# A graph attention layer on one core: TensorE's products in another order within a step

## The chip, the cores and the metric

One core of one Trainium2 chip runs the kernel. A core has TensorE (PE: matmuls and turnings; its weight loads are listed apart as PEld), VectorE (DVE), ScalarE (ACT), GpSimd (POOL) and SyncE (SP), each with an instruction stream of its own that runs in order. DMA transfers are issued from SP, ACT and POOL. PE works on a grid that can be used whole or cut into tiles (64 or 32 rows or columns); the profile writes the tile's shape beside each product (`64*128`: 64 rows, 128 columns). Matmul results land in PSUM, which has eight banks; one bank holds 512 float32 for each of 128 partitions.

The metric is the device time of one launch in microseconds (us).

## The reference, cut to what matters

12500 nodes with 128 channels, 400000 edges sorted by target; `edge_dst` is skewed (its density falls with the node's number).

```python
h = relu(layernorm(x))
msg_src = h @ w_src + b_src
msg_dst = h @ w_dst
message = msg_src[edge_src] + msg_dst[edge_dst]
rad_w = silu(silu(edge_scalars @ w1 + b1) @ w2 + b2) @ w3 + b3     # 32 -> 64 -> 64 -> 128
message = message * edge_attr * rad_w
message = message @ w_sep + b_sep                                  # 128 -> 256
msg_h = message.reshape(n_edges, 8, 16 + 16)
alpha, value = smooth_leaky_relu(msg_h[:, :, :16]), msg_h[:, :, 16:]
score = einsum('ehk,ahk->eh', alpha, alpha_dot)
att = segment_softmax(score, edge_dst)                             # by target node
out = segment_sum(value * att, edge_dst).reshape(n_nodes, 128)
return x + out @ w_proj + b_proj
```

## The kernel before

Three parts follow one another. The first computes the two node tables `t_src` and `t_dst` in DRAM (to about 113 us). The second, `windows()`, goes over the edges in 400 steps of 1000 edges and is nearly the whole run. The third divides, projects and adds the residual (the last 85 us or so).

Within `windows()`, a step `k` handles two sections (f = 0, 1) of 500 edges; a section is four tiles of 125 edges. `step(k)` is a list of calls written by hand; the scheduler is off (`tc.manual_schedule()`), so each engine carries out its instructions in the order in which the calls stand. What a step does, with the lines of the kernel before:

- `gather` (L744, POOL): four indirect DMAs a section fetch the 125 source rows of each tile from `t_src` into `gs0` or `gs1`, each with two buffers. The indices stand in `idx`.
- `sources` (L808, PE): turns the four tiles of a section into PSUM bank `pm0` or `pm1`. `message` (L816, PE) adds the target rows to the same banks: a one-hot matrix `ohT` (L788, DVE) times the window's rows `md`, split into three bfloat16 parts `m3` (`split_md`: L730 and L735 on ACT, L733 and L737 on DVE).
- the radial network: `e_T` (L754) turns the edge scalars, `mlp1` (L763), `mlp2` (L778) and `mlp3` (L795) are products on PE with a silu on ACT between them (L766, L781); L799 (DVE) adds the bias and multiplies by the edge weight: `rad`. Then L821 (DVE) makes the message `mT` from `pm` and `rad`.
- `alphas` (L825 PE, L827 ACT, L829 DVE), a section at a time, through the one bank `pa`.
- `scores` (L836 PE, L839 ACT) every second step, for two steps at once. The scores of eight steps go to DRAM (`sc_d`, L841) and come back laid out by heads (`S`, L846).
- the softmax of a group of eight steps: a scan upwards (L857), one downwards (L862), a subtraction (L867) and an exponential (L869), then four turnings (`softmax_T`, L880) into `Pem`.
- `values` (L908 PE, L910 DVE): `mT` of step c times `w_v`, in bank `V`, times the softmax's numerators, into `pvx`. `one_hot` (L895, L898, DVE) builds the matrix `oh` of the window's targets; `sums` (L919 PE, L923 ACT) adds up by target; `store_win` and `store` (L927, L931, SP) write the result to DRAM.

Values lag the message by LAG = 12 steps (`c = k - LAG`), because the softmax of eight steps must be complete first. PSUM's eight banks are `p3` (two), `pm0`, `pm1`, `V`, `pa`, `misc` and `m1`, each with one buffer; whoever fills a bank waits until its last reader is done. `p3` is shared by all three layers of the radial network, `misc` by scores, sums, `softmax_T` and the index turnings (`prep_make`, L697).

After step 399 the group's last steps run in a tail of LAG + 2 steps, with jobs between them that join windows (`jobs`, from step 401 on).

Of the kernel before, what the change touches and what calls it, by code (L numbers as in the profile page):

```python
# [21 lines left out]
F32 = mybir.dt.float32  # L22
# [30 lines left out]
LAG = 12  # L53
# [3 lines left out]
def gnn_kernel(ctx: ExitStack, tc: tile.TileContext, a: dict, out: bass.AP):  # L57
# [603 lines left out]
    def windows():  # L661
# [5 lines left out]
        with tc.tile_pool(name="wk2", bufs=2) as sp, tc.tile_pool(name="ps", bufs=1, space=PSUM) as pp, \  # L667
# [3 lines left out]
            eTs, h1s, h2s, ohT, m3, mr, mTs, als, S_all, sms, Ps, Pem, pvx, ohs, accs, xs, Ms, pms = (  # L671
                {} for _ in range(18))
# [15 lines left out]
            def prep_make(u):  # L688
                ri, rb = prep[u]
                rows = lp.tile([P, 2, T], F32, name="rows", bufs=1)  # L690
                rf = lp.tile([P, 1], F32, name="rf", bufs=1)
                nc.vector.tensor_copy(rf, rb)
                nc.vector.tensor_copy(rows[:, 0, :], ri[:, 0, :])
                nc.vector.tensor_scalar(rows[:, 1, :], ri[:, 1, :], rf, None, op0=ALU.subtract)
                pt = pp.tile([T, 2, P], F32, name="misc")
# [6 lines left out]
                nc.vector.tensor_copy(loc, pt[:, 1, :])  # L702
                prep[u] = (idx, loc)
# [87 lines left out]
            def mlp3(k):  # L791
                p3 = pp.tile([C, 2, BANK], F32, name="p3")
                for f in range(2):
                    s = slice(f * FC, (f + 1) * FC)
                    nc.tensor.matmul(p3[:, f, 0:SEC], w3b[s, :], h2s[k][s, :], start=True, stop=True)  # L795
                rad = sp.tile([C, PR], F32, name="rad", bufs=1)
# [4 lines left out]
                return rad  # L801
# [9 lines left out]
            def message(k, rad):  # L811
                pm = [pms.pop((k, f)) for f in range(2)]
                for j in range(3):
                    for f in range(2):
                        s = slice(f * W, (f + 1) * W)
                        nc.tensor.matmul(pm[f], m3[k][s, j, :], ohT[k][s, :], start=False, stop=(j == 2),  # L816
                                         skip_group_check=True)
                mTs[k] = sp.tile([C, PR], F32, name="mT", bufs=LAG + 1)
                for f in range(2):
                    s = slice(f * SEC, (f + 1) * SEC)  # L820
                    nc.vector.scalar_tensor_tensor(mTs[k][:, s], pm[f], b_n, rad[:, s], op0=ALU.add, op1=ALU.mult)  # L821

            def alphas(k, f):
                pa = pp.tile([C, SEC], F32, name="pa")
                nc.tensor.matmul(pa, w_a, mTs[k][:, f * SEC:(f + 1) * SEC], start=True, stop=True)  # L825
# [59 lines left out]
            def weights(c):  # L885
                pvx[c] = sp.tile([T, 2, TS, ROW], F32, name="pvx")
                q = c % MP * 2
                for f in range(2):
                    nc.scalar.copy(pvx[c][:, f, :, C:ROW], Pem[c // MP][:, :, q + f, :])

            def one_hot(c):
                _, loc = prep[c // 16]
                ohs[c] = sp.tile([T, 8, W], F32, name="oh")
# [58 lines left out]
            prep_make(0)  # L952
            for k in range(2):
                load_e(k)
            def step(k):
                c = k - LAG
                if has(c - 1):
                    store_win(c - 1)
                    store(c - 1, 0)
# [11 lines left out]
                if has(c - 1):  # L971
                    store(c - 1, 1)
# [3 lines left out]
                if k % 16 == 8 and has(k + 8):  # L976
                    prep_make((k + 8) // 16)
# [5 lines left out]
                if has(k + 1):  # L983
                    split_md(k + 1, 0)
                if has(c):
                    weights(c)
                rad = mlp3(k) if has(k) else None
# [179 lines left out]
            for k in range(NP, NP + LAG + 2):  # L1167
# [167 lines left out]
```

## Time and profile before

| what | us |
|---|---|
| median of 3 runs (4452.02 to 4453.61) | 4452.02 |
| the profiled execution | 4452.25 |
| its span, first to last instruction | 4450.5 |
| first gather starts, last gather starts | 118.7, 4232.1 |
| PE busy | 4148.3 |
| POOL busy | 3117.5 |
| DVE busy | 3083.0 |
| ACT busy | 1957.6 |
| mean granted TensorE clock | 0.981 |

How it is read: busy time is the time in which an engine carried out instructions; the issuing of DMAs by SP and ACT, register work and waits are not in it. A row of a group of instructions gives their line, engine, operation, the tiles written and read, how many there are, then their busy time, the mean of one in ns, and the engine's idle time just before them with what ended it. `issue` means that the profile shows nothing that the engine waited for. In an order of time a row is a start, a length, an engine, a line and an operation, with the idle time before it in brackets.

### The profile page before, as it was taken

The page shows a single profiled execution, that of the slowest core. Times are in us where ns is not written, and L with a number is a line of the kernel's source. Part 1 is how long each engine was busy: PE and PEld are TensorE (multiplying, and loading weights), DVE is VectorE, ACT ScalarE, POOL GpSimd, SP SyncE. Part 2 cuts the span into 40 slices and gives each one's busy share as a digit, 9 for nine tenths or more (in the row PEclk, how much of TensorE's full clock was granted, in tenths as well). Part 3 has the DMA queues.
Part 4 walks back from the last instruction along what each step waited for, and adds up shares of the span by engine and source line. Part 5 has one row for each costly group of instructions (what it writes and reads, how often), then busy time and mean ns, then how long its engine had stood idle before and what let it go on. Part 6 is the DMA issues. An engine that isn't in the chain of part 4 may idle for free.

```text
span 4450.5 us, 87691 instructions
## 1 busy us (share of the span) xinstructions
PE 4148.3 (93%) x29692; PEld 2314.3 (52%) x29692; DVE 3083.0 (69%) x6005; ACT 1957.6 (44%) x4595; POOL 3117.5 (70%) x3223
## 2 busy tenths in 40 slices
PE   6689999999999999999999999999999999999964
PEld 4245555555555555555555555555555555555553
DVE  6367777776776777777777777767767677777666
ACT  5244444444444444444444444444444444444421
POOL 0767777777777777777777777777777777777701
PEclk9799999999999999999999999999999999999987
DMA  5767777777777777777777777776776777777624
GB/s 208 202 179 173 183 186 177 187 184 181 187 178 188 187 178 187 188 177 185 189 177 187 186 172 180 178 178 178 172 183 177 175 181 178 173 182 178 169 51 183
DMA packets 601335, 794.74 MB, mean 179 GB/s; under 512 B 130270, under 2 KB 476974, under 8 KB 600746
## 3 DMA queue, kind: packets, MB, share of 16 engines
q1 hardware_dynamic: 394664, 520.94, 40.9%
q0 software_dynamic: 102816, 210.37, 23.7%
q10 hardware_dynamic: 103394, 57.74, 5.1%
q8 instruction: 234, 3.83, 0.4%
q14 instruction: 227, 1.86, 0.1%
HBM read 648.39 MB, written 140.67 MB: 177 GB/s over the span
## 4 chain that ended last, share of the span: by engine, by line
PE 80%; DVE 8%; ACT 5%; DMA 4%; issue 3%; SPq 1%; POOL 0%; ACTq 0%; POOLq 0%; DVEq 0%
PE V L908 16%; PE pa L825 15%; PE misc L919 8%; PE p L795 8%; PE pm L808 8%; PE pm L816 6%; PE p L763 5%; PE misc L836 5%; PE p L778 4%; PE m L754 2%; ACT sl L827 2%; DVE al L829 2%; DVE M L862 1%; DMA agg<-ob 1%; DVE mT L821 1%
## 5 line engine op out<-in xcount | busy, mean ns | idle before, releaser
L744 POOL DMA_INDIRECT gs<-t_src,idx x3200 | 3103.1, 970 | 1127.8 <-issue 838.5
L827 ACT ACTIVATE sl<-pa,c_b_a 128x500 f32<-128x500 f32 x800 | 543.0, 679 | 1764.4 <-PE pa L825 1760.8
L799 DVE SCALAR_TENSOR_TENSOR rad<-p,c_fc_b,w_b 128x500 f32<-128x500 f32 x800 | 553.3, 733 | 541.0 <-PE p L795 537.7
L829 DVE SCALAR_TENSOR_TENSOR al<-pa,sl 128x500 f32<-128x500 f32 x800 | 543.1, 679 | 551.6 <-ACT sl L827 530.3
L825 PE MATMUL pa<-mT,c_w_a 128*128 128x500 f32 x1600 | 825.4, 597 | 71.2 <-DVE al L829 38.3
L908 PEld LDWEIGHTS V<-c_w_v,mT 128*125 128x125 f32 x6208 | 735.6, 187 | 286.8 <-issue 160.8
L908 PE MATMUL V<-c_w_v,mT 128*125 128x128 f32 x6208 | 883.6, 285 | 0.3
L910 DVE TENSOR_TENSOR pvx<-V,Pem 125x512 f32<-125x512 f32 x776 | 532.0, 686 | 101.8 <-PE V L908 92.1
L821 DVE SCALAR_TENSOR_TENSOR mT<-pm,c_b_src,rad 128x500 f32<-128x500 f32 x800 | 553.1, 733 | 5.9 <-PE pm L816 5.9
L808 PEld LDWEIGHTS pm<-ident,gs 125*128 125x128 f32 x3200 | 352.9, 141 | 314.1 <-issue 251.4
L808 PE MATMUL pm<-ident,gs 125*128 125x125 f32 x3200 | 499.7, 278 | 9.3 <-DMA gs<-t_src,idx 9.3
L919 PE MATMUL misc<-pvx,oh 125*64 125x136 f32 x6400 | 463.4, 287 | 35.9 <-DVE oh L898 35.9
L919 PEld LDWEIGHTS misc<-pvx,oh 125*64 125x64 f32 x6400 | 361.1, 137 | 183.7 <-DVE oh L898 143.9
L795 PE MATMUL p<-h,w3b 64*128 64x500 f32 x1600 | 447.8, 636 | 3.1 <-ACT h L781 3.1
L816 PE MATMUL pm<-ohT,m 64*128 64x500 bf16 x2400 | 325.1, 377 | 0.0
L781 ACT ACTIVATE h<-p,b 128x500 f32<-128x500 f32 x400 | 292.0, 730 | 12.3 <-PE p L778 12.3
L825 PEld LDWEIGHTS pa<-mT,c_w_a 128*128 128x128 f32 x1600 | 239.8, 189 | 101.7 <-DVE al L829 51.9
L766 ACT ACTIVATE h<-p,b 128x500 f32<-128x500 f32 x400 | 289.8, 725 | 0.7 <-PE p L763 0.7
L763 PE MATMUL p<-eT,w1b 64*128 64x250 f32 x1600 | 278.6, 425 | 1.0 <-ACT eT L756 1.0
L778 PE MATMUL p<-h,w2b 64*64 64x250 f32 x3200 | 262.9, 399 | 13.2 <-ACT h L766 13.2
L763 PEld LDWEIGHTS p<-eT,w1b 64*128 64x128 f32 x1600 | 121.0, 185 | 296.4 <-issue 294.6
L895 DVE TENSOR_TENSOR oh<-lane,loc 125x504 f32<-125x504 f32 x400 | 275.1, 688 | 0.0
(145 smaller groups left out, 3138.5 us busy)
## 6 DMA issues: line engine op xcount, KB each, us to landing
w_b<-in_edge_weight SPq DMA_DIRECT2D x400, 500.0 KB
d_b<-in_dst SPq DMA_DIRECT2D x400, 250.0 KB
gs<-t_src,idx POOLq DMA_INDIRECT x3200
e_t<-in_edge_attr ACTq DMA_DIRECT2D x400, 125.0 KB
sc_d<-Sp SPq DMA_DIRECT2D x200, 250.0 KB
win<-ob SPq DMA_DIRECT2D x400, 68.0 KB
agg<-ob SPq DMA_DIRECT2D x800, 33.5 KB
md<-t_dst SPq DMA_DIRECT2D x800, 32.0 KB
```

What stands on the lines that cost most here:

```text
L744: nc.gpsimd.indirect_dma_start(out=gs[:, j, :], out_offset=None, in_=t_src[:, :], in_offset=bass.IndirectOffsetOnAxis(ap=idx[:, t:t + 1], ...
L763: nc.tensor.matmul(p1[:, q, 0:2 * T], w1b[s, :], eTs[k][s, :], start=True, stop=True)
L795: nc.tensor.matmul(p3[:, f, 0:SEC], w3b[s, :], h2s[k][s, :], start=True, stop=True)
L799: nc.vector.scalar_tensor_tensor(rad[:, s], p3[:, f, 0:SEC], b3, w_g[k][:, s], op0=ALU.add, op1=ALU.mult)
L808: nc.tensor.matmul(pms[k, f][:, t * T:(t + 1) * T], gs[:T, t, :], ident[:T, :T], start=(t == 0), stop=False, is_transpose=True, skip_group ...
L816: nc.tensor.matmul(pm[f], m3[k][s, j, :], ohT[k][s, :], start=False, stop=(j == 2), skip_group_check=True)
L821: nc.vector.scalar_tensor_tensor(mTs[k][:, s], pm[f], b_n, rad[:, s], op0=ALU.add, op1=ALU.mult)
L825: nc.tensor.matmul(pa, w_a, mTs[k][:, f * SEC:(f + 1) * SEC], start=True, stop=True)
L827: nc.scalar.activation(sl, pa, AF.Silu, bias=b_a, scale=1.0)
L829: nc.vector.scalar_tensor_tensor(al, pa, 0.25, sl, op0=ALU.mult, op1=ALU.add)
L908: nc.tensor.matmul(V[:, t, :], mTs[c][:, o:o + T], w_v, start=True, stop=True)
L919: nc.tensor.matmul(acc[f * W:(f + 1) * W, :], ohs[c][:, f * TS + t, :], pvx[c][:, f, t, :], start=(t == 0), stop=(t == TS - 1), skip_group ...
```

## The change

No product, vector operation or transfer is added or removed, with one exception: the first layer's silu is two operations of half the size. The order of the calls in `step(k)` is another, and with it the lags:

- `values(c, 0)` and `values(c, 1)` stand half a step apart, each followed by `alphas` of the step before (k - 1) and `sources` of this step, so that three products of the whole grid follow one another; `e_T` is put behind the second three. `mlp1` and `mlp3`, both of 64 rows, follow one another. A step changes the tile's shape six times (seven with scores).
- Both turnings of a step's sources are made in the step itself, half a step apart; before, that of f = 0 was made in the step ahead. The gathers follow them.
- `alphas` comes one step behind the message, `scores` two, `values` 13 (LAG = 13), `sums` 14. The stores follow the sums (`c - 2`), and the tail has LAG + 3 steps. The softmax's parts stand one step later within the group of eight (r = 2, 3, 4).
- `mlp1` writes into the banks `m1` and `misc` in place of `p3`, with a silu for each; `scores` goes to `m1` in place of `misc`.
- `prep_make` is cut in two: the vector operations one step earlier, the turning (`prep_turn`) where it was. `mlp3` and `alphas` are cut into their product and their DVE part (`radial`, `alphas_sum`), which are placed apart. Buffers: `al` 7 for 6, `pvx` 3 for 2.

```diff
-LAG = 12
+LAG = 13
...
-                p1 = pp.tile([P, 2, BANK], F32, name="p3")
+                p1 = [pp.tile([P, 2 * T], F32, name=n) for n in ("m1", "misc")]
                 for q in range(2):
                     s = slice(q * 2 * RAD, (q + 1) * 2 * RAD)
-                    nc.tensor.matmul(p1[:, q, 0:2 * T], w1b[s, :], eTs[k][s, :],
-                                     start=True, stop=True)
+                    nc.tensor.matmul(p1[q], w1b[s, :], eTs[k][s, :], start=True, stop=True)
                 h1s[k] = sp.tile([P, SEC], F32, name="h1")
-                nc.scalar.activation(h1s[k].rearrange("x (f p q) -> x q f p", f=2, q=2),
-                                     p1[:, :, 0:2 * T].rearrange("x q (f p) -> x q f p", f=2),
-                                     AF.Silu, bias=b12[:, 0:1], scale=1.0)
+                h1v = h1s[k].rearrange("x (f p q) -> x q f p", f=2, q=2)
+                for q in range(2):
+                    nc.scalar.activation(h1v[:, q], p1[q].rearrange("x (f p) -> x f p", f=2),
+                                         AF.Silu, bias=b12[:, 0:1], scale=1.0)
...
-                al = sp.tile([C, SEC], F32, name="al", bufs=6)
+                return pa, sl
+
+            def alphas_sum(k, f, pa, sl):
+                al = sp.tile([C, SEC], F32, name="al", bufs=7)
                 nc.vector.scalar_tensor_tensor(al, pa, 0.25, sl, op0=ALU.mult, op1=ALU.add)
...
-                ps = pp.tile([P, SEC], F32, name="misc")
+                ps = pp.tile([P, SEC], F32, name="m1")
...
-                if has(c - 1):
-                    store_win(c - 1)
-                    store(c - 1, 0)
+                if has(c - 2):
+                    store_win(c - 2)
+                    store(c - 2, 0)
...
                 if has(c):
                     weights(c)
-                rad = mlp3(k) if has(k) else None
+                    values(c, 0)
+                if has(k - 1):
+                    sl = alphas(k - 1, 0)
+                if has(k):
+                    sources(k, 0)
+                if has(k + 2):
+                    gather(k + 2, 0)
+                if has(k + 1):
+                    split_md(k + 1, 1)
+                if has(c):
+                    one_hot(c)
+                if has(k - 1):
+                    alphas_sum(k - 1, 0, *sl)
+                if has(k + 1):
+                    split_md(k + 1, 2)
+                if has(k + 2):
+                    mlp1(k + 2)
+                if has(k):
+                    mlp3(k)
+                if has(k + 1):
+                    one_hot_T(k + 1)
+                if has(k):
+                    radial(k)
+                if has(c):
+                    values(c, 1)
+                if has(k - 1):
+                    sl = alphas(k - 1, 1)
                 if has(k):
                     sources(k, 1)
                 if has(k + 2):
                     gather(k + 2, 1)
-                if has(k):
-                    message(k, rad)
-                if has(c):
-                    values(c, 0)
-                if has(k + 1):
-                    split_md(k + 1, 1)
-                if has(k):
-                    alphas(k, 0)
+                if has(k + 3):
+                    e_T(k + 3)
                 if has(k + 6) and k >= -4:
                     load_e(k + 6)
                 if has(k + 1):
-                    split_md(k + 1, 2)
-                if has(k + 2):
-                    mlp1(k + 2)
-                if has(c):
-                    values(c, 1)
-                    one_hot(c)
-
-                if has(k + 1):
-                    sources(k + 1, 0)
-                if has(k + 3):
-                    gather(k + 3, 0)
+                    split_md(k + 1, 3)
+                if has(k - 1):
+                    alphas_sum(k - 1, 1, *sl)
                 if has(k):
-                    alphas(k, 1)
+                    message(k)
+                if has(c - 1):
+                    sums(c - 1)
                 if has(k + 1):
                     mlp2(k + 1)
-                    one_hot_T(k + 1)
-                    split_md(k + 1, 3)
-                if has(c):
-                    sums(c)
-                m, r = divmod(k, MP)
+                if has(k - MP) and r == 4:
+                    softmax_T(m - 1)
+                if has(k - 2) and k % 2 == 1:
+                    scores(k - 2)
                 if has(k - MP):
-                    if r == 1:
+                    if r == 2:
                         softmax_up(m - 1)
-                    elif r == 2:
+                    elif r == 3:
                         softmax_down(m - 1)
                         softmax_exp(m - 1)
-                    elif r == 3:
-                        softmax_T(m - 1)
-                if has(k + 3):
-                    e_T(k + 3)
-                if has(k) and k % 2 == 1:
-                    scores(k)
...
-            for k in range(NP, NP + LAG + 2):
+            for k in range(NP, NP + LAG + 3):
```

More of the change, by code (lines that the diff above doesn't have):

```diff
@@ L670, in windows @@
             prep, e_g, d_g, w_g, md, gath = {}, {}, {}, {}, {}, {}
-            eTs, h1s, h2s, ohT, m3, mr, mTs, als, S_all, sms, Ps, Pem, pvx, ohs, accs, xs, Ms, pms = (
-                {} for _ in range(18))
+            eTs, h1s, h2s, ohT, m3, mr, mTs, als, S_all, sms, Ps, Pem, pvx, ohs, accs, xs, Ms, pms, p3s, rads = (
+                {} for _ in range(20))
             def prep_load(u):
@@ L694, in prep_make, with prep_turn @@
                 nc.vector.tensor_scalar(rows[:, 1, :], ri[:, 1, :], rf, None, op0=ALU.subtract)
+                prep[u] = rows
+            def prep_turn(u):
+                rows = prep[u]
                 pt = pp.tile([T, 2, P], F32, name="misc")
@@ L791, in mlp3, with radial @@
             def mlp3(k):
-                p3 = pp.tile([C, 2, BANK], F32, name="p3")
+                p3s[k] = pp.tile([C, 2, BANK], F32, name="p3")
                 for f in range(2):
                     s = slice(f * FC, (f + 1) * FC)
-                    nc.tensor.matmul(p3[:, f, 0:SEC], w3b[s, :], h2s[k][s, :], start=True, stop=True)
-                rad = sp.tile([C, PR], F32, name="rad", bufs=1)
+                    nc.tensor.matmul(p3s[k][:, f, 0:SEC], w3b[s, :], h2s[k][s, :], start=True, stop=True)
+            def radial(k):
+                p3 = p3s.pop(k)
+                rads[k] = rad = sp.tile([C, PR], F32, name="rad", bufs=1)
                 for f in range(2):
@@ L809, in sources, with message @@
                                      start=(t == 0), stop=False, is_transpose=True, skip_group_check=True)
-            def message(k, rad):
-                pm = [pms.pop((k, f)) for f in range(2)]
+            def message(k):
                 for j in range(3):
@@ L815, in message @@
                         s = slice(f * W, (f + 1) * W)
-                        nc.tensor.matmul(pm[f], m3[k][s, j, :], ohT[k][s, :], start=False, stop=(j == 2),
+                        nc.tensor.matmul(pms[k, f], m3[k][s, j, :], ohT[k][s, :], start=False, stop=(j == 2),
                                          skip_group_check=True)
+                rad = rads.pop(k)
                 mTs[k] = sp.tile([C, PR], F32, name="mT", bufs=LAG + 1)
@@ L820, in message @@
                     s = slice(f * SEC, (f + 1) * SEC)
-                    nc.vector.scalar_tensor_tensor(mTs[k][:, s], pm[f], b_n, rad[:, s], op0=ALU.add, op1=ALU.mult)
+                    nc.vector.scalar_tensor_tensor(mTs[k][:, s], pms.pop((k, f)), b_n, rad[:, s],
+                                                   op0=ALU.add, op1=ALU.mult)
             def alphas(k, f):
@@ L885, in weights @@
             def weights(c):
-                pvx[c] = sp.tile([T, 2, TS, ROW], F32, name="pvx")
+                pvx[c] = sp.tile([T, 2, TS, ROW], F32, name="pvx", bufs=3)
                 q = c % MP * 2
@@ L892, in one_hot @@
                 _, loc = prep[c // 16]
-                ohs[c] = sp.tile([T, 8, W], F32, name="oh")
+                ohs[c] = sp.tile([T, 8, W], F32, name="oh", bufs=2)
                 t0 = c % 16 * 8
@@ L952, in windows @@
             prep_make(0)
+            prep_turn(0)
             for k in range(2):
@@ L970, in step @@
                     load_sm((k + 4) // MP)
-                if has(c - 1):
-                    store(c - 1, 1)
+                if has(c - 2):
+                    store(c - 2, 1)
                 if 0 <= 2 * k < NZ:
@@ L976, in step @@
                 if k % 16 == 8 and has(k + 8):
-                    prep_make((k + 8) // 16)
+                    prep_turn((k + 8) // 16)
+                if k % 16 == 7 and has(k + 9):
+                    prep_make((k + 9) // 16)
                 i, q = divmod(k - 40, MP)
@@ L984, in step @@
                     split_md(k + 1, 0)
+                m, r = divmod(k, MP)
                 if has(c):
                     weights(c)
[L987 removed]
+                    values(c, 0)
[25 more added lines that the diff above has]
+                    sl = alphas(k - 1, 1)
                 if has(k):
```

1 line of the change is left out of this document (removed).

## The prediction

> **What bounds the kernel now.** I read the page first (engine shares and the chain of waits), then POOL's gather line with all that it waited for, then PE's order of time in one step, then DVE beside POOL.
>
> From the page (shares of the span; the chain by engine; the costliest group, with its busy time, mean ns and the idle time before it):
>
> ```profile
> PE 4148.3 (93%) x29692; PEld 2314.3 (52%) x29692; DVE 3083.0 (69%) x6005; ACT 1957.6 (44%) x4595; POOL 3117.5 (70%) x3223
> PE 80%; DVE 8%; ACT 5%; DMA 4%; issue 3%; SPq 1%; POOL 0%; ACTq 0%; POOLq 0%; DVEq 0%
> L744 POOL DMA_INDIRECT gs<-t_src,idx x3200 | 3103.1, 970 | 1127.8 <-issue 838.5 <-DVE loc L702 116.5 <-PE pm L808 50.6
> ```
>
> Read alone, this says that PE is the bound and POOL has 30% to spare. The gather line by itself says otherwise (duration min/median/max, first and last start; then what ended POOL's idle time, us and times):
>
> ```profile
> L744 POOL DMA_INDIRECT gs<-t_src,idx x3200: 941/947/1537, 118.7 to 4232.1; - x189
> ...
>   issue: 838.5, 2745
> ...
>   PE pm L808: 50.6, 61
> ```
>
> 838.5 / 2745 = 0.305 us stands before every gather with no releaser, so a gather costs POOL 0.970 + 0.305 = 1.275 us. 3200 of them are 4080 us; from 118.7 to 4232.1 + 0.95 there are 4114. Only about 34 us are left in which POOL waited for PE: 50.6 less 61 x 0.305 is 32, and a row `PE misc L836: 4.8, 10` adds 1.7. In three stretches of 164 us (16 steps, 128 gathers each) POOL is busy 124.5 us on average, and 128 x 0.305 = 39.0 more makes 163.5. POOL is full, and PE is ahead of it by next to nothing: two engines bound this loop at once.
>
> PE in one step without scores (start, us, then idle time where there was any):
>
> ```profile
> 2510.34 1.11 PE L795 MATMUL p<-h,w3b 64*128 64x500 f32 x4
> 2511.38 0.65 PE L808 MATMUL pm<-ident,gs 125*128 125x125 f32 x4
> 2511.96 0.81 PE L816 MATMUL pm<-ohT,m 64*128 64x500 bf16 x6
> ...
> 2516.23 0.59 PE L808 MATMUL pm<-ident,gs 125*128 125x125 f32 x4
> 2516.66 1.01 PE L825 MATMUL pa<-mT,c_w_a 128*128 128x500 f32 x2
> ...
> 2519.26 0.43 PE L754 MATMUL m<-ident,e_t 125*128 125x125 f32 x2
> 2519.62 1.11 PE L795 MATMUL p<-h,w3b 64*128 64x500 f32 x4
> ```
>
> No idle time; 9.28 us from one L795 to the next, and 10.33 in the step before it, which has scores (2500.01 to 2510.34). The same four turnings L808 take 0.58 us between neighbours of another tile shape (64 rows) and 0.43 between neighbours of their own: 0.15 us for a change.
>
> DVE beside POOL, two pairs from one order of time:
>
> ```profile
> 4221.54 0.67 DVE L895 TENSOR_TENSOR oh<-lane,loc 125x504 f32<-125x504 f32 x1
> 4221.63 1.40 POOL L744 DMA_INDIRECT gs<-t_src,idx  x1 [0.30 <-issue]
> ...
> 4230.82 0.73 DVE L895 TENSOR_TENSOR oh<-lane,loc 125x504 f32<-125x504 f32 x1
> 4230.84 0.95 POOL L744 DMA_INDIRECT gs<-t_src,idx  x1 [0.30 <-issue]
> ```
>
> In the first the one-hot is under way when the gather starts, has 0.58 us to go, and the gather takes 0.45 us longer than 0.95. In the second both start together and the gather keeps its 0.95. The gathers' mean over their fast value, 970 - 944 = 26 ns, times 3200 is 82 us of such meetings.
>
> **The change, part by part.**
>
> *PE's order.* No product is added or taken out. A step has nine changes of shape before (ten with scores), six (seven) after: 3 x 0.15 = 0.45 us a step, 8.83 and 9.88 us, 9.36 on average. Bounds: nothing, if not the change but something else makes L808 longer, and twice as much, since L808 is short. I take 0.45. With what a group of 16 steps has besides (164 - 8 x 9.28 - 8 x 10.33 = 7 us of softmax turnings, index turnings and waits) PE then needs about 157 us for 16 steps, POOL 128 x 1.275 = 163. PE's gain of 180 us over 400 steps is therefore cut off after the 34 us that POOL waited. Two of these waits, 8.05 us at 232 and 2.10 us at 249, less 0.3 each, fall in the filling of the pipeline behind a late load and stay: **-24 us** (bounds 0 and -34).
>
> *First layer into two banks (m1, misc), two silus in place of one.* One more ACT operation a step, under 0.7 us, on an engine busy 44%: nothing. If ACT were late, the next e_T would wait, and PE has 0.4 us a step in hand.
>
> *Alphas a step later, scores two, values 13, sums 14.* Their inputs are ready a step earlier than needed; buffers grow with them (al 7, pvx 3, mT 14). SP's stores go a step later with the sums; the order of its other issues stays. Each set of four gathers is still issued right behind the turning that frees its buffer, two steps ahead of its use. Nothing in the loop.
>
> *Softmax.* The scores of a group now end at step 8m+9 and the running maximum stands at the end of 8m+10: one step, 9 us or more, for the way through DRAM, where two were. DVE stands behind that wait with the next pvx, and PE behind DVE. The trace does not show S landing. Bounds: the read is issued 2.2 us after the last score write (2449.34 and 2451.52), because it waits for that to land; and the scan found S in place 17.7 us after the scores (2449.3 and 2467.1). The read has the write's size, 250 KB, so I take another 2.2 and some room: 5 us. Cost nothing; what it costs beyond 9 us is a rival.
>
> *DVE's order.* The same operations with the same durations, but mr now stands right before the two one-hots, ohT before the radial, the scans behind mT. Their meetings with gathers fall anew. Of the operations with no PSUM operand, one of d us that meets gathers at random (pitch 1.275, the last 0.1 us free) costs (d - 0.1)^2 / 2.55: one-hot 0.688: 0.136 x 400 = 54 us; ohT 0.475: 22; the two subtractions of the split, 0.28 each: 11; 100 scans of 1.194: 47; 50 subtractions of 0.68: 7; the rest 4. Sum 145, against 82 measured: the old order met fewer than chance. Bounds: 0 (every op meets its gather as at 4230.82), and 235 (one-hot hit in full in every step, 400 x 0.588). POOL now sets the pace and PE follows landings that scatter, so meetings blur toward chance; but the ops are the measured ones, so I stay near the measured row: 90, **+8 us**.
>
> *Ends.* The last gather ends at 4233.04 and PE takes that set at 4244.03. With PE waiting for gathers the lead of 11 us falls to a landing. The very first gather, issued at 118.7, is taken at 124.46 after a wait, 4.8 us after POOL is done with it, among many other transfers; bounds 0 and 8, I take 4: -7 us. One more step in the tail is +4.6 (pm L908 at 4257.33 and 4261.97); sums there no longer wait 1.55 us for oh, which I count in the two or three early steps that no store holds, -4. Together **-6 us** (bounds -16 and +12).
>
> Sum: 4450.5 - 24 + 8 - 6 = 4428.5 us of span; the profiled run had 1.75 us around its span (4452.25), and it stands 0.2 over the median of 4452.02. Predicted 4430, 0.5% faster. From no change it can be told at 0.2%, 9 us.
>
> **The rivals.**
>
> 1. *POOL's gap is elastic* and PE's whole gain arrives: 180 us less, about 4275. For it: the chain gives PE 80% and POOL 0%. Against: 0.305 us stands before 2745 of 3200 gathers, whoever is late. 0.05.
> 2. *Meetings with DVE grow*, the other side. Place: POOL, at gathers that start under a one-hot or a scan. At chance, 145 - 82 = +63, the total is 4450.5 - 24 + 63 - 6 + 1.75 = 4485; with the one-hot locked into each step 4575. It decides from 121 us of meetings on (39 more: 24 + 6 + 9). For it: the new adjacency and pacing. Against: PE's landings scatter, 82 is the measured row. 0.20. The Trainium skill (SBUF — State Buffer, section Who interferes with whom) states that a VectorE operation with two SBUF inputs contends with GpSimd operations that read SBUF, and that the loser blocks fully. The 1.40 us gather agrees; that the gather holds off VectorE for its whole length does not show, as the one-hot at 4230.82 lost 0.06 us. By the rule alone meetings come at chance, the 4485 above.
> 3. *Softmax's maximum waits for S.* If S lands 17 us after the scores, DVE and then PE wait some 7.5 us in each group of eight steps. PE's 78.5 us a group become 86, POOL's are 81.6: 50 x 4.4 = 220 us more, about 4650. For it: two steps became one. Against: the write of the same size landed in 2.2 us. 0.05.
> 4. *PE gets no shorter* (the change does not do what it says: what L808 loses lies in weight loads, not shapes). POOL goes on waiting: 4445 to 4462. 0.12.
>
> **How the numbers follow.** Forecast 0.58, rivals as above. The forecast's own range is the collisions' 50 to 125 and the ends: 4385 to 4475. Of its 0.58, 0.47 are faster than 4443, 0.09 within, 0.02 slower; rival 1 is faster; of rival 2 0.17 are slower and 0.03 within; rival 3 slower; rival 4 0.07 within, 0.04 slower, 0.01 faster. Faster 0.53, same 0.19, slower 0.28. The range takes in rival 2 at chance and leaves out 1 and 3: 4385 to 4500.
>
> **What would show it.** Right: PE pm L814 (the turnings) waits for `DMA gs` some hundreds of times, 200 us or more in all; `PE pm L814` almost vanishes from POOL's waits; gathers 0.30 apart throughout; first to last gather about 4098. The L814 before alphas takes 0.5 us or less and a step's products sum to about 8.8 us. The gathers' mean over 944 ns, times 3200, gives the meetings: 90 or not. Wrong: POOL gaps other than 0.30 (rival 1), a mean over 980 ns (2), DVE waiting at L867 (3), no PE wait for gathers (4).

## The result and the profile after

| what | before | after |
|---|---|---|
| median (4 runs each, side by side), us | 4452.82 | 4415.2 |
| ratio to before, 95% interval | | 0.9915 (0.9897 to 0.9932) |
| span of the profiled execution, us | 4450.5 | 4414.9 |
| first gather starts, last gather ends, us | 118.73, 4233.04 | 117.27, 4208.71 |
| mean granted TensorE clock | 0.981 | 0.961 |

The changed kernel is 0.85% faster, 38 us by the medians; the prediction was 4430 us. On the page of the changed kernel the shares of the engines, the chain by engine and by line, and the two groups that matter (busy time, mean ns, idle time before and what ended most of it) read:

```profile
PE 4015.5 (91%) x29692; PEld 2440.7 (55%) x29692; DVE 3092.6 (70%) x6005; ACT 2080.8 (47%) x4995; POOL 3111.1 (70%) x3223
...
PE 57%; DMA 21%; POOL 10%; issue 6%; DVE 3%; SPq 1%; ACT 1%; POOLq 0%; ACTq 0%; DVEq 0%
DMA gs<-t_src,idx 16%; PE V L918 11%; POOL gs L748 10%; PE pa L832 9%; PE misc L929 7%; PE pm L814 6%; PE pm L821 5%; PE p L799 5%; PE m L767 4%; PE p L782 4%; PE m L846 3%; DMA agg<-ob 3%; PE m L758 1%; DMA e_t<-in_edge_attr 1%; PE misc L890 1%
...
L748 POOL DMA_INDIRECT gs<-t_src,idx x3200 | 3096.7, 968 | 1109.8 <-issue 815.9
...
L814 PE MATMUL pm<-ident,gs 125*128 125x125 f32 x3200 | 533.8, 276 | 210.6 <-DMA gs<-t_src,idx 198.8
```

The busy shares have hardly moved. The chain has: POOL and the landing of its gathers hold 26% of it, where POOL had 0% and DMA 4%. What POOL waited for in the changed kernel (us and times):

```profile
L748 POOL DMA_INDIRECT gs<-t_src,idx x3200: 938/944/1905, 117.3 to 4207.8; - x189
...
  issue: 815.9, 2675
...
  PE pm L814: 47.0, 98
```

Of the 47.0 us, 98 x 0.305 = 29.9 are the gap that stands before every gather; 17 are left, and 14.4 of these are a single wait. In the steady loop POOL no longer waits for PE. PE waits instead, as the view of PE's waits shows (us, times, longest):

```profile
PE pm L814 <- DMA gs<-t_src,idx: 198.8, 191, 5.7
```

One step of PE without scores and without a wait, in the order of time:

```profile
2503.64 1.04 PE L918 MATMUL V<-c_w_v,mT 128*125 128x128 f32 x8
2504.52 1.00 PE L832 MATMUL pa<-mT,c_w_a 128*128 128x500 f32 x2
2505.36 0.59 PE L814 MATMUL pm<-ident,gs 125*128 125x125 f32 x4
...
2506.41 1.00 PE L799 MATMUL p<-h,w3b 64*128 64x500 f32 x4
2507.34 1.14 PE L918 MATMUL V<-c_w_v,mT 128*125 128x128 f32 x8
2508.32 1.00 PE L832 MATMUL pa<-mT,c_w_a 128*128 128x500 f32 x2
...
2512.39 1.14 PE L918 MATMUL V<-c_w_v,mT 128*125 128x128 f32 x8
```

From one first `V` to the next are 8.75 us, where a step of the kernel before took 9.28. The row from which the prediction took its price, the turnings, gave little of this: from their start to the next row it is 0.52 us, where L808 between 64-row products took 0.58. More came from products that lost a neighbour of another shape: `alphas` takes 0.84 us to the next row (2504.52 to 2505.36), where it took 0.93 (2516.66 to 2517.59), and the third layer 0.93 (2506.41 to 2507.34), where it took 1.04 (2510.34 to 2511.38). Yet 16 steps still take 163.0 us on average (164.3 before), which is 128 gathers at 0.968 + 0.305 us: POOL's pace.

The one long wait of POOL has its own story, in the order of time around 260 us (SP's issues are marked SPq):

```profile
249.53 0.35 SPq L851 DMA_DIRECT2D sc_d<-Sp  x1
...
259.38 0.55 SPq L856 DMA_DIRECT2D S<-sc_d  x1
...
262.95 1.20 DVE L867 TENSOR_TENSOR_SCAN M<-sm,S 128x500 f32<-128x500 bf16 x1 [18.83 <-DMA S<-sc_d]
...
268.11 0.94 POOL L748 DMA_INDIRECT gs<-t_src,idx  x1 [14.67 <-PE pm L814]
```

In the first group of eight steps the read of the scores is issued 9.85 us after the last write, not the 2.2 of the steady loop, DVE stands 18.8 us at the scan, PE behind it, and POOL behind PE.

Where the 35.6 us of span came from: from the start of the first gather to the end of the last 4091.4 us against 4114.3, so -22.9 (POOL's waits beyond its 0.305 us some -16.4, the gathers' own time -6.4); the first gather 1.5 us earlier; after the last gather 206.1 us against 217.4, so -11.3.

The -6.4 us are not fewer meetings with DVE. The median gather took 947 ns in the profile of the kernel before and 944 in this one, which is 9.6 us over 3200 gathers. Either length occurs with either order (944 in e3, e4 and, with the old order, e13; 947 in e8 and e12), so it can't be put down to the change; why it differs stays open. Counted over its own median, what meetings add went from 73 to 76 us.

### The profile page after: what moved, and what is told of

Same layout as the page of the kernel before. It is cut to its first block, busy times and chain, and to the rows that moved or that the text cites. A ratio compares the mean times of both kernels' runs of the same rounds, so it can differ in the third digit from the quotient of the medians.

```text
span 4414.9 us, 88298 instructions
## 1 busy us (share of the span) xinstructions
PE 4015.5 (91%) x29692; PEld 2440.7 (55%) x29692; DVE 3092.6 (70%) x6005; ACT 2080.8 (47%) x4995; POOL 3111.1 (70%) x3223
## 4 chain that ended last, share of the span: by engine, by line
PE 57%; DMA 21%; POOL 10%; issue 6%; DVE 3%; SPq 1%; ACT 1%; POOLq 0%; ACTq 0%; DVEq 0%
DMA gs<-t_src,idx 16%; PE V L918 11%; POOL gs L748 10%; PE pa L832 9%; PE misc L929 7%; PE pm L814 6%; PE pm L821 5%; PE p L799 5%; PE m L767 4%; PE p L782 4%; PE m L846 3%; DMA agg<-ob 3%; PE m L758 1%; DMA e_t<-in_edge_attr 1%; PE misc L890 1%
## 5 line engine op out<-in xcount | busy, mean ns | idle before, releaser
L814 PEld LDWEIGHTS pm<-ident,gs 125*128 125x128 f32 x3200 | 408.9, 142 | 676.8 <-issue 392.3
L814 PE MATMUL pm<-ident,gs 125*128 125x125 f32 x3200 | 533.8, 276 | 210.6 <-DMA gs<-t_src,idx 198.8
L929 PE MATMUL misc<-pvx,oh 125*64 125x136 f32 x6400 | 479.4, 294 | 0.0
L929 PEld LDWEIGHTS misc<-pvx,oh 125*64 125x64 f32 x6400 | 374.5, 141 | 170.2 <-ACT eT L760 143.3
L799 PE MATMUL p<-h,w3b 64*128 64x500 f32 x1600 | 414.7, 596 | 9.3 <-ACT h L785 9.3
L785 ACT ACTIVATE h<-p,b 128x500 f32<-128x500 f32 x400 | 325.8, 815 | 183.4 <-PE p L782 143.9
L933 ACT COPY ob<-misc 128x136 f32<-128x136 f32 x400 | 109.0, 273 | 638.3 <-PE misc L929 524.5
L821 PE MATMUL pm<-ohT,m 64*128 64x500 bf16 x2400 | 336.7, 388 | 0.0
L767 PE MATMUL m<-eT,w1b 64*128 64x250 f32 x800 | 280.3, 431 | 3.8 <-ACT Sp L849 2.8
L767 PE MATMUL misc<-eT,w1b 64*128 64x250 f32 x800 | 280.3, 431 | 0.0
```

Of the source, the lines that this page charges most:

```text
L767: nc.tensor.matmul(p1[q], w1b[s, :], eTs[k][s, :], start=True, stop=True)
L799: nc.tensor.matmul(p3s[k][:, f, 0:SEC], w3b[s, :], h2s[k][s, :], start=True, stop=True)
L814: nc.tensor.matmul(pms[k, f][:, t * T:(t + 1) * T], gs[:T, t, :], ident[:T, :T], start=(t == 0), stop=False, is_transpose=True, skip_group ...
L821: nc.tensor.matmul(pms[k, f], m3[k][s, j, :], ohT[k][s, :], start=False, stop=(j == 2), skip_group_check=True)
L929: nc.tensor.matmul(acc[f * W:(f + 1) * W, :], ohs[c][:, f * TS + t, :], pvx[c][:, f, t, :], start=(t == 0), stop=(t == TS - 1), skip_group ...
```

## The experiments

Every time is compared with the kernel before on the same chip. The theory is that of the prediction: POOL's gathers, 1.275 us from start to start, set the pace of the changed kernel, and PE's larger gain is cut off there.

**Fewer gathers, before and after (e1, e2).** The same edit in both kernels; the source rows of a quarter of the edges are left out.

```diff
-                for j in range(TS):
+                for j in range(TS - 1):
                     t = k % 16 * 8 + f * TS + j
...
-                    nc.tensor.matmul(pms[k, f][:, t * T:(t + 1) * T], gs[:T, t, :], ident[:T, :T],
+                    nc.tensor.matmul(pms[k, f][:, t * T:(t + 1) * T], gs[:T, min(t, TS - 2), :], ident[:T, :T],
```

> The kernel before with three gathers for each set of four; the turning of the fourth tile turns the third again (left out: the source rows of a quarter of the edges). POOL then needs 2400 x 1.275 = 3060 us. Theory (PE and POOL bound the loop of before together, PE ahead of POOL by next to nothing): PE alone sets the pace, its 16 steps stay at 164 us, and the time falls by 0 to 25 us only, to 4427 to 4452. Rival (before was bound by POOL with PE well ahead): a fall of 100 us or more.

> The same in the changed kernel (left out: the source rows of a quarter of the edges). Theory: the new order made PE some 0.45 to 0.52 us a step shorter, 180 to 208 us, and POOL hid it; without the fourth gather it shows: 4230 to 4285, 180 us or more under the kernel before with three gathers. Rival (PE's order of products is worth only what was seen): 36 us under that kernel, about 4400.

Measured: e1 4444.93 us, ratio 0.9990 (0.9981 to 0.9999); e2 4146.22, ratio 0.9318 (0.9303 to 0.9332), the kernel before at 4449.37. The gather's row on the page of e1, then of e2:

```profile
L744 POOL DMA_INDIRECT gs<-t_src,idx x2400 | 2513.8, 1047 | 1709.4 <-PE pm L808 1054.4
```

```profile
L748 POOL DMA_INDIRECT gs<-t_src,idx x2400 | 2320.3, 967 | 1611.6 <-PE pm L814 787.5
```

In both POOL now waits for PE, so it is no longer POOL that sets the time. The old order needs almost the same time with a quarter of POOL's work gone (4.4 us less): PE's side of the loop had no room. The new one loses some 266 us at once (by the ratios, 0.9915 and 0.9318). Between e1 and e2 lie 299 us, 0.75 us a step; the theory had expected 180 to 208. A step of e2 without scores, from one L799 to the next:

```profile
2511.75 1.00 PE L799 MATMUL p<-h,w3b 64*128 64x500 f32 x4
...
2520.50 1.00 PE L799 MATMUL p<-h,w3b 64*128 64x500 f32 x4
```

These are 8.75 us, and 9.73 with scores, against 9.28 and 10.33; 16 steps take 151.9 us against 164.3. Of these 12.4 us, 9.0 are the steps' products (8 x 0.53 and 8 x 0.60), 2.5 are waits of PE that e1 has and e2 has not (4.9 and 2.4), and some 0.9 the turnings of softmax and indices. The rival "worth only what was seen" (4400) is out.

**PE made slower (e3).** The first layer's products stand between two turnings, which puts two changes of shape back.

```diff
                 if has(k):
-                    sources(k, 0)
+                    sources(k, 0, range(2))
+                if has(k + 2):
+                    mlp1(k + 2)
+                if has(k):
+                    sources(k, 0, range(2, TS))
```

> The changed kernel with the first layer's products put between the second and the third turning of the first set: two changes of tile shape more in each step, 0.3 us, 120 us of PE's time, the same products. Theory (POOL sets the pace, PE has 6 us in hand in 16 steps and loses 4.8): the same time as the changed kernel within 10 us, 4405 to 4425. Rival (PE sets the pace): 4535.

Measured: 4403.93 us, ratio 0.9901 (0.9887 to 0.9916), the same as the changed kernel's 0.9915 within the intervals; the rival's 4535 us is out. In the order of time of e3:

```profile
2502.57 1.14 PE L919 MATMUL V<-c_w_v,mT 128*125 128x128 f32 x8
...
2509.34 0.38 PE L815 MATMUL pm<-ident,gs 125*128 125x125 f32 x2
2509.65 0.47 PE L767 MATMUL m<-eT,w1b 64*128 64x250 f32 x1
...
2510.27 0.43 PE L815 MATMUL pm<-ident,gs 125*128 125x125 f32 x2
2510.63 1.11 PE L799 MATMUL p<-h,w3b 64*128 64x500 f32 x4
2511.67 1.14 PE L919 MATMUL V<-c_w_v,mT 128*125 128x128 f32 x8
```

The step takes 9.10 us, 0.35 more for two changes of shape, or 0.18 each: 140 us over 400 steps. The time does not show them. Most of them came out of PE's waits for gathers, which were 198.8 us in the changed kernel and in e3 are:

```profile
PE pm L815 <- DMA gs<-t_src,idx: 92.2, 89, 4.7
```

**Shorter one-hots (e4).**

```diff
-                nc.vector.tensor_tensor(
-                    ohs[c][:, :, 0:W - 1], lane[:T, 0:W - 1].unsqueeze(1).to_broadcast([T, 8, W - 1]),
-                    loc[:, t0:t0 + 8].unsqueeze(2).to_broadcast([T, 8, W - 1]), op=ALU.is_equal)
+                for o in range(0, 8, 2):
+                    nc.vector.tensor_tensor(
+                        ohs[c][:, o:o + 2, 0:W - 1], lane[:T, 0:W - 1].unsqueeze(1).to_broadcast([T, 2, W - 1]),
+                        loc[:, t0 + o:t0 + o + 2].unsqueeze(2).to_broadcast([T, 2, W - 1]), op=ALU.is_equal)
```

> The changed kernel with the one-hot of a step made by four operations of two tiles each instead of one of eight: more VectorE time, shorter operations. Theory (POOL sets the pace, and a gather that starts under a one-hot of 0.69 us is lengthened by what is left of it): the 31.6 us of meetings under the one-hot in the changed kernel's trace fall to about 5, the gathers' mean from 968 to 960 ns, and the time by 20 to 30 us, to about 4390. Rival (POOL's length does not set the time): no change, or slower by the extra VectorE work.

Measured: 4403.68 us, ratio 0.9897 (0.9882 to 0.9912), 8 us below the changed kernel by the ratios and not to be told from it. The expected 20 to 30 us did not come, and by its time alone e4 does not speak against the rival. The gathers' mean fell from 968 to 965 ns only, where 960 was expected:

```profile
L748 POOL DMA_INDIRECT gs<-t_src,idx x3200 | 3088.6, 965 | 1108.0 <-issue 812.2
```

Put down to the DVE operation under which a gather starts, what gathers take over 944 ns went from 31.6 to about 9 us at the one-hot, where 5 were expected. But at the target's one-hot `ohT` (L792), which follows on DVE, it went from 0.5 to 15.3 us. One such meeting in e4:

```profile
776.63 0.47 DVE L792 TENSOR_SCALAR ohT<-d_b,tgt 128x500 bf16<-128x500 int32 x1
776.77 1.15 POOL L748 DMA_INDIRECT gs<-t_src,idx  x1 [0.30 <-DVE al L839]
```

The gather starts with 0.33 us of the operation to go and takes 0.20 longer than 0.95. In e4 `ohT` meets 98 gathers that take over 960 ns, in the changed kernel 3: the one-hot in four parts takes longer in all, and `ohT` behind it has moved under the gathers. The sum over all operations fell from 76 to 68 us.

**All of them short, and the first scan later (e7, e10, e12).** One-hot in four parts as in e4, `ohT` in two, both scans in four (each carried on from the last column of the part before), and the first group's forward scan a step later:

```diff
-                    if r == 2:
+                    if r == 2 and m > 1:
                         softmax_up(m - 1)
                     elif r == 3:
+                        if m == 1:
+                            softmax_up(m - 1)
                         softmax_down(m - 1)
```

> The changed kernel with shorter VectorE operations (one-hot in four, the target's one-hot in two, each scan in four), and the first group's forward scan one step later. Theory (POOL sets the pace; a gather is lengthened by what is left of the operation it starts under): one-hot 31.6 to 8 us of meetings, scans 37.6 to 8, the target's one-hot up to 10; all meetings 76 to about 35; and the one wait of 14.7 us at 268 us falls by some 10: about 50 us below the changed kernel, 4350 to 4375. Rival (meetings only move to other operations): within 15 us of the changed kernel, about 4400.

> The same kernel as e7 (the changed kernel with short VectorE operations and the first group's scan a step later), again for the same reason. In the trace of e7 the meetings are 36.9 us, 39 less than in the changed kernel. Theory (POOL sets the pace): 39 from the meetings and some 10 from the one wait at 268 us, 50 us below the changed kernel: 4355 to 4375, ratio to before about 0.981. Rival (POOL's length is not the time): a ratio of 0.99 as in the changed kernel.

> The same kernel as e7 and e10, a third time, in the hope of a chip on which the kernel before takes 4450 us and not 5843. There: theory (POOL sets the pace) 39 us less meetings and some 10 less of the one early wait than the changed kernel, 4355 to 4375, ratio about 0.981; rival (POOL's length is not the time) a ratio of 0.99. Where the kernel before takes 5843 us, POOL is not the pace-maker and both give the 0.962 to 0.967 seen before.

e5 to e8 ran on one chip and e9 and e10 on another on which the kernel before took 5844 and 5843 us, 31% more than elsewhere. There e7 took 5645.52 us, ratio 0.9617 (0.9563 to 0.9671), and e10 5660.09, ratio 0.9673 (0.9639 to 0.9706). Neither says anything on the theory, which needs a POOL that sets the pace. From the order of time of e9 on such a chip:

```profile
2500.39 1.14 PE L908 MATMUL V<-c_w_v,mT 128*125 128x128 f32 x8
...
2501.70 1.11 PE L825 MATMUL pa<-mT,c_w_a 128*128 128x500 f32 x2 [0.17 <-issue]
...
2505.35 0.69 DVE L910 TENSOR_TENSOR pvx<-V,Pem 125x512 f32<-125x512 f32 x1 [3.06 <-issue]
...
2506.83 0.68 ACT L827 ACTIVATE sl<-pa,c_b_a 128x500 f32<-128x500 f32 x1 [7.06 <-remote]
```

DVE takes up `V` 3.8 us after PE is done with it, and ACT `pa` 4.0 us after. Why these engines stand there no record shows; it stays open.

e12, on a chip where the kernel before took 4450.29 us, is the run that bears on the theory: 4386.53 us, ratio 0.9861 (0.9845 to 0.9877). It beats both kernels: 0.5% under the changed one (the intervals do not touch), 1.4% under the kernel before. The page of e12, then its DVE waits and POOL waits:

```profile
L748 POOL DMA_INDIRECT gs<-t_src,idx x3200 | 3072.0, 960 | 1104.2 <-issue 801.8
```

```profile
DVE M L869 <- DMA S<-sc_d: 17.8, 5, 9.3
```

```profile
POOL gs L748 <- PE pm L815: 49.8, 122, 11.0
```

First to last gather took 4060.2 us, 31.2 less than in the changed kernel, with more DVE work (7905 operations for 6005). Of these, 24.7 are the gathers' own time (968 to 960 ns in the mean) and some 6.5 POOL's waits. So the length of POOL's gathers does set the time. The expected 50 us were too much. The meetings fell by 34 us, each profile counted over its own median gather, rather than by 39 to 41, and 9.6 of it are hidden, as the median gather took 947 ns in this profile and 944 in that of the changed kernel. The early wait fell from 14.67 to 11.02 us only: DVE's wait for `S` was halved, but `al` stands behind the scans and PE behind `al`.

**The first scan alone (e8), six changes of shape (e6).** e8 is the edit just shown, in the changed kernel; e6 puts each of the four products of the first and third layers behind one turning:

```diff
+                for t in range(TS):
+                    if has(k):
+                        sources(k, 0, range(t, t + 1))
+                    if t < 2 and has(k + 2):
+                        mlp1(k + 2, t)
+                    if t == 2 and has(k):
+                        mlp3(k, 0)
...
-                    mlp3(k)
+                    mlp3(k, 1)
```

> The changed kernel with the forward scan of the first group alone one step later, behind the one-hot and the message of that step. Theory (VectorE's wait of 18.8 us for the scores at 263 us, with the zeroing of the sums in the same queues, holds PE and then POOL once for 14.7 us): POOL's wait there falls to 2 to 6 us, the time by 8 to 13 us, to about 4400. Rival (the wait is made up for behind it): no change, 4411.

> The changed kernel with the four products of 64 rows of the first and third layer each put behind one turning of the first set: six changes of shape more in each step instead of two, the same products. By the run with two (9.104 us a step against 8.750: 0.177 us each) PE's 16 steps are 151.9 + 16 x 1.06 = 168.9 us, above POOL's 163.0. Theory (the slower of the two sets the pace): 25 x 5.9 = 147 us more than the changed kernel, about 4555 (4500 with 0.15 us a change). Rival (the gathers' chain alone sets the pace, PE's order is of no account): 4400 to 4415.

Both fell on the chip of e5: e8 5581.58 us, ratio 0.9532 (0.9480 to 0.9584), e6 6864.09, ratio 1.170 (1.162 to 1.178). Neither decides its question. The row of e8's page shows that POOL was not the pace-maker there:

```profile
L748 POOL DMA_INDIRECT gs<-t_src,idx x3200 | 3088.4, 965 | 2257.7 <-PE pm L814 912.6
```

That six changes of shape would push PE past POOL at 4555 us is therefore not shown. Nor would e6 have been a clean test elsewhere. In the changed kernel the two products of the third layer start together (2506.41 both), in the two halves of the grid, and take 0.93 us to the next row. In e6 each stands alone behind a turning and takes 1.03 us (2508.19 to 2509.22, 2509.48 to 2510.51). From the first turning to `V` it is 4.27 us (2506.24 to 2510.51) where the changed kernel takes 1.98 (2505.36 to 2507.34), so the edit costs PE 2.3 us a step and not the 1.06 expected: it takes away the products' overlap as well.

**The kernel before with lighter messages (e5, e9, e13).** Two of the three parts of the target features are left out, and with them four of the six products of `message` in a step.

```diff
-                for j in range(3):
+                for j in range(1):
...
-                        nc.tensor.matmul(pm[f], m3[k][s, j, :], ohT[k][s, :], start=False, stop=(j == 2),
+                        nc.tensor.matmul(pm[f], m3[k][s, j, :], ohT[k][s, :], start=False, stop=(j == 0),
```

> The kernel before with two of the message's six products left out of each step (left out: the second and third bf16 parts of the target features), four of 64x500 less at 0.735 / 6 each: PE 0.49 us a step shorter, 196 us in all, and nothing else moved. Theory (PE's shortening is all that the change brings, and POOL cuts it off): the time falls by what the whole change brought, 27 to 37 us, to about 4417. Rival (PE alone sets the pace): 4253. Rival (the lags, the softmax or VectorE's order bring the gain): no fall, 4440 to 4450.

> The same kernel as e5 (before, four of 64x500 products of the message left out of each step, the second and third bf16 parts of the target features), again, because the kernel before took 5844 us on the chip of e5 to e8 instead of 4450 and PE stood there in gaps that no record explains. Theory: 27 to 37 us less than before, as much as the whole change. Rival (PE alone sets the pace): 196 us less. Rival (lags, softmax or VectorE's order bring the gain): no fall.

> The same kernel as e5 and e9 (before without the message's second and third bf16 parts of the target features: four products of 64x500 less in a step, PE 0.49 us a step shorter and nothing moved), a third time. On a chip where the kernel before takes 4450 us: theory (PE's shortening is all that the change brings, and POOL cuts it off) 27 to 40 us less, 4410 to 4423, ratio 0.991 to 0.994, with PE waiting for gathers in place of POOL for PE; rival (PE alone sets the pace) 196 us less, 4254; rival (the lags, the softmax or VectorE's order bring the gain) no fall. On a chip where it takes 5843 us: again no fall.

On the two chips where the kernel before took 5844 and 5843 us: 5839.45, ratio 0.9974 (0.9933 to 1.0015), and 5867.47, ratio 1.0024 (0.9992 to 1.0055). e13, with the kernel before at 4450.43: 4447.68 us, ratio 0.9994 (0.9985 to 1.0003). No fall: the expectation failed, and the number is that of the third rival (the lags, the softmax or VectorE's order bring the gain). The waits of PE in e13, then the same place in the order of time of the kernel before and of e13:

```profile
PE pa L825 <- DVE mT L821: 112.5, 397, 1.2
```

```profile
2500.01 1.11 PE L795 MATMUL p<-h,w3b 64*128 64x500 f32 x4
...
2503.34 1.03 PE L825 MATMUL pa<-mT,c_w_a 128*128 128x500 f32 x2
```

```profile
2504.41 1.11 PE L795 MATMUL p<-h,w3b 64*128 64x500 f32 x4
...
2505.57 1.39 DVE L799 SCALAR_TENSOR_TENSOR rad<-p,c_fc_b,w_b 128x500 f32<-128x500 f32 x2 [2.09 <-PE p L795]
...
2506.03 0.39 PE L816 MATMUL pm<-ohT,m 64*128 64x500 bf16 x2
...
2506.87 1.38 DVE L821 SCALAR_TENSOR_TENSOR mT<-pm,c_b_src,rad 128x500 f32<-128x500 f32 x2
...
2507.65 1.10 PE L825 MATMUL pa<-mT,c_w_a 128*128 128x500 f32 x2 [0.17 <-DVE mT L821]
```

The message's products became 0.42 us shorter, but `alphas` of the same step needs `mT`, and `mT` needs `rad`: from L795 to L825 it is 3.24 us by way of DVE, and it had been 3.33 by way of PE (2500.01 to 2503.34 in the kernel before). A second chain lay 0.09 us behind PE's own there, so most of what was taken from PE between these two products came back as a wait (397 of them, one in nearly every step). The rest went too: behind the wait, `alphas` takes 1.03 us to the next row (2507.65 to 2508.68), where it took 0.96 (2503.34 to 2504.30). The step still takes 9.27 us. This answers for the place, not for the theory: it shows that the old order could not be sped up at that place, whatever POOL had to give. The change moves `alphas` a step behind the message, and in its trace PE waits at `pa` for `al` 23 times in the whole run. So the gain is that of the order and the lag together. Whether the order of shapes without that lag would have gained anything was not tried, and the third rival is not out as far as the lag goes.

## Why the prediction was right, step by step

- **What bounds the kernel.** "POOL is full, and PE is ahead of it by next to nothing: two engines bound this loop at once" held: with a quarter of the gathers gone the old kernel loses 4.4 us (e1), with shorter gathers and a later first scan the new one loses about 24 (e12, by the ratios). What the reading left out is the chain from the third layer by `rad` and `mT` to `alphas`, 0.09 us behind PE in the step shown (e13).
- **Alphas a step later: "Nothing in the loop".** It costs nothing, but e13 suggests that it does something: in the old place, PE's shortening came back as a wait at `alphas`. The sum is untouched, since the change brings order and lag together; how much each brings is open.
- **PE's order: 3 x 0.15 = 0.45 us a step.** Right in kind, too small: 0.53 and 0.60 us, and 0.75 to 0.78 with the waits that went too. The price came from a row that hardly moved; `alphas` and the third layer gave more than the turnings (which stand behind `alphas` in the new order, and not before it, as the prediction's last paragraph has it). A change of shape put back cost 0.18 (e3). PE needs 151.9 us for 16 steps, not 157. As POOL's 163 cut off the rest, the error did not reach the time.
- **POOL's waits on PE: -24.** The 24 us of the steady loop went, all but 2. In the filling of the pipeline the waits grew from about 11 to 18, where the prediction let them stay: -16 on balance.
- **Softmax: nothing.** Right for the groups of the steady loop (four waits at the scan in the whole run), wrong for the first: there the way through DRAM took more than the one step that was left, and 14.4 us were lost. It is rival 3's mechanism, once instead of 50 times. The zeroing of the sums is still being issued by SP then (the last at 246.8 us); that it makes the write land late was not tried.
- **Meetings with DVE: +8.** It was +3: 76 us against 73, well inside the bounds of 0 and 235. The prediction's 82 us for the kernel before count from 944 ns, but the median gather of that profile took 947, so 9.6 of them were no meetings. Counted from 944 in both profiles the sum would have fallen, from 82 to 76, but only by the shorter median gather. 69 us of it now lie at one-hot and scans, where before it was 49 at the one-hot with the rest scattered. e4 shows how little can be foreseen here: one operation cut into shorter ones moved the next one under the gathers.
- **Ends: -6.** It was -12.7. The lead of the last set fell from 11.0 to 4.9 us (4208.71 to 4213.56), -6.1 for the -7 predicted; the first gather -1.5. The extra step of the tail was paid for and more: steps of the tail follow at 3.0 us where nothing else holds them, not at 4.64, because sums no longer wait for `oh` in any of them. The prediction counted that for two or three.
- **The sum.** Predicted were -24 + 8 - 6 = -22 us, measured -16 + 3 - 10 - 13, unrounded -35.6: waits 8 short of what was predicted, meetings 5 better, ends 7 better, and 9.6 us by the shorter median gather, a term that the prediction does not have and the change does not explain. These make the 13.6 us between 4428.5 and 4414.9. The path (PE shorter, POOL's waits gone, PE waiting for gathers) came as forecast; that the span fell further than forecast is in part luck.
- **The rivals.** POOL's gap stayed 0.304 to 0.306 us at nearly all gathers (rival 1 out); the meetings grew by 3 us, where rival 2 needed 39; PE did get shorter (rival 4).

## What to carry to other kernels

Two engines that are both full within a few tenths of a per cent show up as one bound and one idle share; add the gap before each instruction to the busy time before believing the idle share, and take work from one of them in an experiment to see what it is worth. A gain on one engine is worth little more than the other's waits, here 38 us where e1 and e2 show 299, and the rest must be fetched where the next bound is: shortening the DVE operations under which gathers start, with the first scan moved, brought some 24 us more. Before taking work off an engine, look for the chain that runs beside it in the same step, and for the first pass of a loop, where a lag that is long enough later may not be.

## What was not expected of the hardware

- A gather is lengthened by a DVE operation that reads one SBUF tensor and a scalar column as well (`ohT`, tensor_scalar, 0.47 us: 1.15 for 0.95), not only by operations with two SBUF inputs. What counts is that the operation is under way when the gather starts, as the two pairs of rows in the prediction show (1.40 us against 0.95). By the Trainium skill (SBUF — State Buffer, section Who interferes with whom) one with a single SBUF input contends only in a two-port mode. Which mode it ran in the trace does not name. What the runs show is that it goes at twice the one-hot's rate: the median `ohT` of 500 columns takes 0.47 us and one of 250 in e12 0.34, so 0.52 ns a column, where the one-hot takes 1.05 (0.68 us for 504 columns, 0.28 for 126 in e4).
- Where PE waits, its granted clock is lower: the mean fell from 0.981 to 0.961 with PE's 198.8 us of waits for gathers. From 250 to 268 us, around the early wait, it was 0.50, and four turnings took 1.04 us at 266.80 and 0.59 at 271.72. What this cost was not measured by itself.
- Two products of 64 rows in the two halves of the grid run side by side (both at 2506.41, 0.93 us to the next row); parted by a turning, each takes 1.03 us (e6).
- The same kernel took 4450 us on some chips and 5843 on two others, with engines standing for microseconds between instructions. There the run nearest to the changed kernel (e8) was 4.7% faster than before, and the version with more and shorter DVE operations, the best elsewhere, did not beat it (0.9617 and 0.9673 against 0.9532).
